# The local transformer of a twelve-layer kernel, with its instruction order given as cyclic lists per engine

## The chip, the core and the metric

The kernel runs on one core of a Trainium2 chip. TensorE (PE) multiplies matrices and writes to PSUM, whose eight banks hold 128 x 512 float32 each; VectorE (DVE), ScalarE (ACT) and GpSimd (POOL) work element by element; SyncE (SP) issues the DMAs. Each engine works through its own instructions in order and waits on semaphores for the others. The metric is the time of one execution in microseconds on the device, as a median of several runs.

## The reference

Everything is float32; activations are (8, 256, 128). Twelve layers of four families follow each other, each added to its input: mixture of experts, attention, mixture of experts; two-branch feed-forward, RWKV-6, two-branch feed-forward; **local transformer**, attention, **local transformer**; mixture of experts, attention, mixture of experts. The change touches only the two local transformers. Each runs six layers (`DEPTH = 6`) of this, with 16 heads of 64 and windows of 32:

```python
def attn_layer(x, Wqkv, qs, ksc, Wo):
    q, k, v = split(x @ Wqkv)                     # 128 -> 3 x 1024
    q = l2norm(q) * qs
    k = l2norm(k) * ksc
    q = q * cos * scale + rotate_half(q) * sin * scale
    k = k * cos * inv + rotate_half(k) * sin * inv
    # each window of 32 queries looks at its own and the previous 32 keys
    sim = einsum('bhwie,bhwje->bhwij', q, k2) * 8 ; mask ; softmax
    return einsum('bhwij,bhwje->bhwie', attn, v2) @ Wo

def ffn_layer(x, g, bln, W1, b1, W2, b2):
    xn = (x - mu) / jnp.sqrt(var + 1e-05) * g + bln
    a, gate = split(xn @ W1 + b1)                 # 128 -> 2 x 341
    return a * gelu(gate) @ W2 + b2

for i in range(DEPTH):
    x = attn_layer(shift_tokens(x), ...) + x      # shift: half the channels move one token
    x = ffn_layer(shift_tokens(x), ...) + x
```

## The kernel before

Channels lie on partitions, tokens along the row. The eight sequences form four groups of two (`NG = 4`), so a tile of activations is 128 x 512. The layers are stages 0 to 11; the local transformers are stages 6 and 8, written by `ffn2`.

In a local stage the work is cut into **quads**: one layer, one group, four of the sixteen heads. Four quads and the output projection and feed-forward behind them are a **unit**; a stage has 6 x 4 = 24 units, 96 quads. A quad is this chain: projection of k and of q (`pp`, `quad_project`), squares on ACT, cosine product and partner shuffle on DVE, sine product and sum on POOL; sums of squares per head on PE (`bank`, `quad_norms`), their inverse roots on ACT (`quad_roots`, an Ln and an Exp), four small DMAs that bring the roots into `l_rt`, shuffles on DVE that spread them (`quad_pick`), scaling of k and q on POOL (`quad_keys`); value projection `vp`, copied on ACT into `l_v` and by two DMAs, moved by one window, into `l_w` (`quad_values`); scores `sc`, maximum and difference on DVE (`quad_scores`); exp on ACT (`quad_exp`); transposes `et`, copied on ACT into `l_at` (`quad_turn`); weighted values `cx` in two halves, each divided on DVE (`quad_weigh`); transposes back `ct`, copied on ACT into `l_ct` (`quad_back`, `quad_done`). Behind the fourth quad of a unit comes `local_rest`: the output projection `wo_acc` in three parts, the residual `x1`, the shift, the normalization (`mean`, `ln_c`, `ln_sq`, `var`, `lv`, `ln_r`, `t` and its affine), the three chunks of W1 with gelu (`ge`, `l_gl`, `l_ag`), W2 (`w_acc`) and the residual `x2`.

The order of the work is the order in which the program is written. `_Ordered` ties each instruction of PE, DVE, ACT and POOL to the one before it on that engine, so no scheduler moves it; the DMAs on SP are not tied. `ffn2` (line 1630) is a loop that takes one new quad per step and writes, in a fixed sequence of whole functions, a part of each of the last four quads: `q0` projections, norms, roots and values; `q1` picking, scaling and scores; `q2` exp, transposes and weighted values; `q3` transposes back. The rest of a unit is a generator whose pieces are written at four places of each step (`piece`), over four steps from the one in which its last quad is transposed back. Two of these places call `pump` where no piece is due or the piece leaves room, which writes the next bit of work of a neighbouring stage (the end of the one before, the normalization at the entrance of the one behind). `entered` calls `pump` until a group's input is there.

In PSUM a local stage has three tiles of two banks (`two`, shared by `pp`, `vp`, `sc`, `et`, `cx`, `ct`, `ge`), one bank for the norms and the pumped work, and one bank for `wo_acc`, `mean`, `var` and `w_acc`.

Because all instructions of a local stage go through `_Ordered`, they carry its line, L285, in the profile; the tile names tell them apart.

Of the kernel before, what the change touches and what calls it, by code (L numbers as in the profile page):

```python
# [28 lines left out]
P = 128  # L29
B, S, D = 8, 256, 128  # L30
NB = 2
# [262 lines left out]
class _Net:  # L294
# [952 lines left out]
    def local_rows(self):  # L1247

        gp = self.nc.gpsimd
        one = lambda n, i, shape: self.work(f"{n}{i}", shape, bufs=1)  # L1250

        self.xs = [one("l_xs", i, (P, T)) for i in range(4)]
        for t in self.xs:
            gp.memset(t[64:, 0::S], 0.0)
        self.n_pad = 0

        self.rt = one("l_rt", 0, (P, T))
        gp.memset(self.rt, 0.0)
        self.low_masks(("lrow", "lmask"))
# [37 lines left out]
    def quad_project(self, q, n):  # L1297

        nc = self.nc
        four = lambda a: a.rearrange("p j (b s) -> p (j b) s", b=NB)  # L1300
        o = S if n == "k" else 0
        pp = self.two("pp")
        for j in range(2):
            self.mm(pp[:, j, :], q.w[:, o + P * j : o + P * (j + 1)], q.xs)
        sq = self.work("l_sq", (P, 2, T), bufs=4)
        nc.scalar.activation(sq, pp, AF.Square)
        y = self.work("l_y" + n, (P, 2, T), bufs=2)
        nc.vector.tensor_tensor(four(y), four(pp), q.tab[n + "cos"], ALU.mult)
        yr = self.work("l_yr", (P, 2, T), bufs=2)
        nc.vector.stream_shuffle(yr, pp, [i ^ 1 for i in range(32)])  # L1310
        nc.gpsimd.tensor_tensor(four(yr), four(yr), q.tab[n + "sin"], ALU.mult)
        nc.gpsimd.tensor_tensor(y, y, yr, ALU.add)
        q.y[n], q.sq[n] = y, sq

    def quad_values(self, q):
        nc = self.nc
        vp = self.two("vp").rearrange("p a b -> p (a b)")
        for m in range(4):
            self.mm(vp[:, S * m : S * (m + 1)], q.xs[:, P * m : P * (m + 1)], q.w[:, 2 * S :])
        v, w = self.vs[q.n % 2]  # L1320
        nc.scalar.copy(v.rearrange("p m h d -> p (m h) d")[:, :, :64],
                       vp.rearrange("p (n d) -> p n d", d=64))
        nc.sync.dma_start(w[32:], v[:96])
        nc.sync.dma_start(w[:32, 1::2], v[96:, 0::2])
        q.v = (w, v)

    def quad_norms(self, q):  # L1330
        sp = self.ps()
        for s, (n, j) in enumerate((("k", 0), ("q", 0), ("k", 1), ("q", 1))):
            self.mm(sp[32 * s : 32 * s + 32, :], self.get("hsum"), q.sq[n][:, j, :])
        q.sums = self.work("l_rn", bufs=1)
        self.nc.vector.tensor_scalar(q.sums, sp, 1e-24, None, ALU.max)

    def quad_roots(self, q):
        nc = self.nc
        rn = q.sums
        self.act(rn, rn, AF.Ln, scale=2.0**SH)  # L1340
        self.act(rn, rn, AF.Exp, bias=self.get("eps", 3, 1), scale=-0.5)
        for s in range(4):
            nc.sync.dma_start(self.rt[s::32], rn[32 * s : 32 * s + 32 : 8, :])

    def quad_pick(self, q):
        nc = self.nc
        q.r = {}
        for n, o in (("k", 0), ("q", 1)):
            r = q.r[n] = self.work("l_sq", (P, 2, T), bufs=4)
            for j in range(2):  # L1350
                nc.vector.stream_shuffle(r[:, j, :], self.rt, [2 * j + o] * 32)

    def quad_keys(self, q):

        nc = self.nc
        q.kp = self.kp[q.n % len(self.kp)]
        seq = lambda a: a.rearrange("p j (b s) -> p (j b) s", b=NB)
        nc.gpsimd.tensor_tensor(q.kp[:, :, WIN:], seq(q.r["k"]), seq(q.y["k"]), ALU.mult)
        nc.gpsimd.tensor_tensor(q.y["q"], q.y["q"], q.r["q"], ALU.mult)

    def quad_scores(self, q):

        nc = self.nc
        sc = self.two("sc")
# [19 lines left out]
        sl = lambda a: a.rearrange("p (n k) -> p n k", k=64)  # L1384
        bc = lambda a: a.unsqueeze(2).to_broadcast([P, 16, 64])
        sv = sl(sc.rearrange("p h n -> p (h n)"))
        mx = self.work("l_mx", (P, 16), bufs=2)
        nc.vector.tensor_reduce(mx, sv, AX.X, ALU.max)
        e = self.work("l_e", (P, 2 * T), bufs=2)
        nc.vector.tensor_tensor(sl(e), sv, bc(mx), ALU.subtract)  # L1390
        q.e = e

    def quad_exp(self, q):
        self.act(q.e, q.e, AF.Exp)

    def quad_turn(self, q):

        nc = self.nc
        tp = self.two("et").rearrange("p a b -> p (a b)")
        for n in range(8):  # L1400
            nc.tensor.transpose(tp[:, P * n : P * (n + 1)], q.e[:, P * n : P * (n + 1)],
                                self.get("ident"))
        q.at = self.work("l_at", (P, 2 * T), bufs=1)
        nc.scalar.copy(q.at, tp)

    def quad_weigh(self, q):

        nc = self.nc
        q.cx = []
        for j in range(2):  # L1410
            cp = self.two("cx")[:, :, : 4 * 65].rearrange("p x (n d) -> p x n d", d=65)
            for b in range(NB):
                for h in range(2):
                    for jj in range(4):
                        for x in range(2):
                            ks = slice(64 * x, 64 * x + 64)
                            o = P * (4 * h + 2 * j + b) + 32 * jj
                            self.mm(cp[32 * jj : 32 * jj + 32, x, 2 * b + h, :],
                                    q.at[ks, o : o + 32],
                                    q.v[jj % 2][ks, 2 * b + jj // 2, 2 * j + h, :])  # L1420
            rc = self.work("l_rc", (P, 2, 4), bufs=2)
            nc.vector.reciprocal(rc, cp[:, :, :, 64])
            cx = self.work("l_cx", (P, 2, 4, 64), bufs=4)
            nc.vector.tensor_tensor(cx, cp[:, :, :, :64],
                                    rc.unsqueeze(3).to_broadcast([P, 2, 4, 64]), ALU.mult)
            q.cx.append(cx)

    def quad_back(self, q):

        nc = self.nc  # L1430
        tp = q.tp = self.two("ct")
        for j in range(2):
            to = tp[:, j, :].rearrange("p (b c x i) -> p b x c i", b=NB, c=2, x=2)
            for b in range(NB):
                for x in range(2):
                    nc.tensor.transpose(
                        to[:, b, x], q.cx[j][:, x, 2 * b : 2 * b + 2].rearrange("p h d -> p (h d)"),
                        self.get("ident"))

    def quad_done(self, q):  # L1440
        ct = self.work("l_ct", (P, 2, T), bufs=5)
        self.nc.scalar.copy(ct, q.tp)
        q.unit.ct.append(ct)

    def local_rest(self, u):


        nc, i = self.nc, u.i
        acc = self.bank1("wo_acc")

        def project(cs):
            for c in cs:
                self.mm(acc, u.w["wo"][:, c, :], u.ct[c // 2][:, c % 2, :], start=c == 0, stop=c == 7)

        project(range(3))
        yield False
        project(range(3, 6))
        yield False
        yield False
        project(range(6, 8))  # L1460
        u.x1 = self.new_x()
        nc.vector.tensor_tensor(u.x1, acc, self.ys[u.g], ALU.add)
        if i == DEPTH - 1 and u.g == NG - 1:
            self.rest = u
            return
        xs = self.shifted(u.x1)
        yield False

        yield False
        self.settle()  # L1470
        xc, r = self.scratch("ln_c"), self.scratch("ln_r")
        m = self.bank1("mean")
        self.mm(m, self.get("mean"), xs)
        nc.vector.tensor_tensor(xc, xs, m, ALU.subtract)
        sq = self.scratch("ln_sq")
        nc.scalar.activation(sq, xc, AF.Square)
        yield True
        yield True
        v = self.bank1("var")
        self.mm(v, self.get("mean"), sq)  # L1480
        self.rsqrt(r, v, 0)

        hn = self.scratch("t", bufs=2)
        u.early = [
            lambda: nc.vector.tensor_tensor(hn, xc, r, ALU.mult),
            lambda: nc.scalar.activation(hn, hn, AF.Identity, bias=self.get(f"F{i}_ln_b"),
                                         scale=self.get(f"F{i}_ln_g")),
        ]
        yield True
        for f in u.early:  # L1490
            f()
        u.early = []
        yield False
        yield True
        o = self.bank1("w2_acc")
        ags = []

        def second(m):
            f = GE_CHUNKS[m][1]
            self.mm(o, u.w["w2"][:f, m, :], ags[m][:f, :], start=m == 0, stop=m == 2)  # L1500

        def first(m):
            f, w = GE_CHUNKS[m]
# [318 lines left out]
```

## Time and profile before

| | |
|---|---|
| median of 3 runs | 5218.47 us (5218.33 to 5227.95) |
| span of the profiled execution, first to last instruction | 5219.8 us |
| stage 6 (local), first to last quad and its rest | about 955 to 2660 us |
| stage 8 (local) | about 2905 to 4600 us |
| PE busy in stage 6, stage 8 | 1609 of 1705 us, 1596 of 1695 us |
| DVE, ACT, POOL busy in stage 6 | 1332, 903, 1397 us |
| granted clock of PE, mean | 0.973 of full speed |

The two local stages are some 3400 of 5220 us. How to read what follows: a row of a timeline gives the start, the duration, the engine, the line and the operation, output tile before input tiles, the shape, and how many instructions were merged; in square brackets stands how long the engine had been idle before it and what ended the wait. A row of busy time by stretch gives for PE, weight loads, DVE, ACT and POOL the busy microseconds and the count of instructions, then the granted clock of PE, the share of the DMA engines and GB/s. A row of a group gives the total busy time, the mean of one in ns, and the idle time in front. A float32 matmul stands as two instructions in the profile.

### The profile page before, as it was taken

The page shows a single profiled execution, that of the slowest core. Times are in us where ns is not written, and L with a number is a line of the kernel's source. Part 1 is how long each engine was busy: PE and PEld are TensorE (multiplying, and loading weights), DVE is VectorE, ACT ScalarE, POOL GpSimd, SP SyncE. Part 2 cuts the span into 40 slices and gives each one's busy share as a digit, 9 for nine tenths or more (in the row PEclk, how much of TensorE's full clock was granted, in tenths as well). Part 3 has the DMA queues.
Part 4 walks back from the last instruction along what each step waited for, and adds up shares of the span by engine and source line. Part 5 has one row for each costly group of instructions (what it writes and reads, how often), then busy time and mean ns, then how long its engine had stood idle before and what let it go on. Part 6 is the DMA issues. An engine that isn't in the chain of part 4 may idle for free.

```text
span 5219.8 us, 156276 instructions
## 1 busy us (share of the span) xinstructions
PE 4887.5 (94%) x70032; PEld 2895.3 (55%) x70032; DVE 3599.4 (69%) x6390; ACT 2483.9 (48%) x3011; POOL 3033.2 (58%) x1543
## 2 busy tenths in 40 slices
PE   9999998899999999999988899999999999989889
PEld 6755764455555555555544455555555555555456
DVE  4445446777777877787745777877787778755655
ACT  2233225555555555555544455555555555543652
POOL 0011003688888887888720588888888888701520
PEclk9999998999999999999989999999999999999999
DMA  2000000111111111111000011111111111100000
GB/s 75 1 1 1 1 1 1 40 29 49 34 49 35 43 38 45 38 42 41 26 28 5 21 36 42 37 46 37 42 41 42 41 39 41 29 36 1 1 1 9
DMA packets 61390, 151.76 MB, mean 29 GB/s; under 512 B 11185, under 2 KB 25394, under 8 KB 60466
## 3 DMA queue, kind: packets, MB, share of 16 engines
q1 hardware_dynamic: 60722, 141.77, 8.9%
q8 instruction: 551, 9.03, 0.7%
q14 instruction: 117, 0.96, 0.1%
HBM read 44.93 MB, written 1.05 MB: 9 GB/s over the span
## 4 chain that ended last, share of the span: by engine, by line
PE 71%; DVE 14%; ACT 8%; issue 2%; POOL 1%; DMA 1%; SPq 1%; DVEq 0%; ACTq 0%; POOLq 0%
PE mm L340 11%; PE pp L285 8%; PE e_o L340 7%; PE wo_acc L285 7%; PE bank L285 6%; PE sc L285 5%; PE vp L285 5%; PE ge L285 5%; PE cx L285 3%; PE ct L285 3%; DVE l_sq L285 3%; PE w_acc L285 2%; DVE l_yr L285 2%; PE ms L285 2%; ACT l_ct L285 2%
## 5 line engine op out<-in xcount | busy, mean ns | idle before, releaser
L285 PE MATMUL pp<-l_xs,wqkv 128*128 128x512 f32 x1536 | 693.4, 594 | 5.5 <-DMA wqkv<-in_f_wqkv 3.8
L285 POOL TENSOR_TENSOR l_kp<-l_sq,l_yk 128x1024 f32<-128x1024 f32 x192 | 456.6, 2378 | 357.4 <-DVE l_sq L285 354.2
L285 ACT COPY l_v<-vp 128x1024 f32<-128x1024 f32 x192 | 194.6, 1014 | 693.5 <-PE vp L285 693.5
L285 DVE STREAM_SHUFFLE l_sq<-l_rt 128x512 f32<-128x512 f32 x768 | 515.7, 747 | 0.1
L285 DVE STREAM_SHUFFLE l_yr<-pp 128x1024 f32<-128x1024 f32 x384 | 510.2, 1329 | 0.0
L285 PEld LDWEIGHTS pp<-l_xs,wqkv 128*128 128x128 f32 x1536 | 292.6, 191 | 356.6 <-issue 327.2
L340 PE MATMUL mm<-x,m 128*128 128x512 f32 x1024 | 479.4, 608 | 0.0
L285 POOL TENSOR_TENSOR l_yq<-l_yq,l_sq 128x1024 f32<-128x1024 f32 x192 | 476.1, 2479 | 0.1
L285 POOL TENSOR_TENSOR l_yr<-l_yr,l_ksin 128x1024 f32<-128x1024 f32 x192 | 456.5, 2378 | 24.9 <-DVE l_yr L285 24.9
L285 POOL TENSOR_TENSOR l_yq<-l_yq,l_yr 128x1024 f32<-128x1024 f32 x192 | 455.0, 2370 | 15.1
L285 POOL TENSOR_TENSOR l_yk<-l_yk,l_yr 128x1024 f32<-128x1024 f32 x192 | 454.2, 2366 | 15.0
L285 POOL TENSOR_TENSOR l_yr<-l_yr,l_qsin 128x1024 f32<-128x1024 f32 x192 | 455.0, 2370 | 0.0
L285 DVE TENSOR_REDUCE l_mx<-sc 128x16 f32<-128x1024 f32 x192 | 235.1, 1225 | 277.1 <-PE sc L285 277.1
L285 ACT ACTIVATE l_sq<-pp 128x1024 f32<-128x1024 f32 x384 | 384.1, 1013 | 54.5 <-PE pp L285 54.2
L340 PEld LDWEIGHTS e_o<-m,e_h 128*128 128x128 f32 x3072 | 363.1, 192 | 60.8 <-issue 60.3
L285 PE MATMUL vp<-wqkv,l_xs 128*128 128x256 f32 x1536 | 388.4, 396 | 2.6 <-issue 1.6
L285 PE MATMUL bank<-l_sq,sb_cs 128*32 128x512 f32 x1536 | 305.0, 617 | 67.0 <-ACT l_sq L285 66.5
L340 PE MATMUL e_o<-m,e_h 128*128 128x128 f32 x3072 | 363.6, 275 | 0.0
L285 PE MATMUL wo_acc<-l_ct,wo 128*128 128x512 f32 x768 | 360.9, 603 | 2.3 <-issue 2.3
L285 PE MATMUL cx<-l_w,l_at 64*32 64x65 f32 x12288 | 312.2, 226 | 51.0 <-ACT l_ct L285 41.1
L285 PE MATMUL sc<-l_kp,l_yq 64*32 64x64 f32 x24576 | 312.2, 228 | 22.6 <-issue 14.3
L285 PE MATMUL cx<-l_v,l_at 64*32 64x65 f32 x12288 | 318.8, 227 | 3.1 <-issue 3.1
(316 smaller groups left out, 9566.9 us busy)
## 6 DMA issues: line engine op xcount, KB each, us to landing
l_w<-l_v SPq DMA_DIRECT2D x192, 390.0 KB
wqkv<-in_f_wqkv SPq DMA_DIRECT2D x48, 384.0 KB
l_w<-l_v SPq DMA_DIRECT2D x192, 65.0 KB
l_rt<-l_rn SPq DMA_DIRECT2D x768, 8.0 KB
wo<-in_f_wo SPq DMA_DIRECT2D x12, 512.0 KB
m<-in_m_w SPq DMA_DIRECT2D x16, 256.0 KB
w<-in_f_w SPq DMA_DIRECT2D x12, 341.0 KB
w<-in_f_w SPq DMA_DIRECT2D x12, 192.0 KB
```

What stands on the lines that cost most here:

```text
L285: r = f(*args, **kw)
L340: self.nc.tensor.matmul(out, lhsT=lhsT, rhs=rhs, start=start, stop=stop)
```

## The change

The work is the same, operation by operation; what is rewritten is the order. Each function of a quad and of a unit's rest is cut into single operations (`op_ppk`, `op_sqk`, `op_cosk` and so on; 36 for a quad, 30 for a unit). `ORDER` gives each engine a cyclic list. `ppk.1` means: in step t this engine does `ppk` of quad t - 1. Operations of a unit exist only for its last quad. `AFTER` says what must have been written before an operation can be written (an operation and how many quads back), `HELD` which operations free the PSUM place that one takes. `ffn2` fills one queue per engine and step and writes from the head of each queue whatever is ready, until nothing moves; then it calls `pump` once. So the program order on each engine is its list, repeated.

```diff
+    ORDER = {
+        "PE": (
+            "ppk.1 mean.6 ppq.1 w20.7 wo1.5 ge2.7 ctp.5 wo0.4 var.6 norms.1 vp.3 cx1.4 "
+            "cx0.4 sc.2 ge1.6 ge0.6 wo2.5 w21.7 et.3"
+        ),
+        "ACT": (
+            "tab1.7 gl1.7 gl0.7 at.4 sqk.1 lsq.6 sqq.1 gl2.7 tab2.7 lln.6 ct.5 lex.6 "
+            "exp.3 v.3 aff.6 rln.1 rex.1 inA.0 xsA.5"
+        ),
+        "DVE": (
+            "x2.8 x1.6 qshuf.2 ag0.7 kshuf.2 xc.6 cosk.1 shufk.1 cosq.1 shufq.1 ag2.7 "
+            "hn.6 nmax.1 d1.4 d0.4 max.2 sub.2 ag1.6"
+        ),
+        "POOL": (
+            "xsP.6 kadd.2 kscale.2 qscale.2 inP.1 ksin.1 qsin.1 qadd.1"
+        ),
+        "DMA": (
+            "vs.4 rt.1"
+        ),
+    }
+    AFTER = {
+        "ppk": "inA.1 inP.1",
...
+        "norms": "sqk.0 sqq.0",
...
+        "at": "et.0 cx0.1 cx1.1",
...
+        "rt": "rex.0 kshuf.1 qshuf.1",
+    }
+    HELD = {
+        "ppk": ("psp2", "sqk cosk shufk"),
...
+        "sc": ("psp2", "sub"),
+        "norms": ("bank", "nmax"),
+        "wo0": ("acc", "x1"),
...
+    }
+    PLACES = {"psp2": 3, "bank": 1, "acc": 1}
...
     def ffn2(self):
...
-        while True:
-            q0 = next(gen, None)
...
-            if q1:
-                self.quad_pick(q1)
-            if q1:
-                self.quad_keys(q1)
...
-            self.piece(pieces, True)
-            q1, q2, q3 = q0, q1, q2
+        t, last = 0, max(k for l in order.values() for _, k in l)
+        while t < total + last or any(queues.values()):
+            for e, l in order.items():
+                queues[e].extend((o, t - k) for o, k in l if exists(o, t - k))
+            moved = True
+            while moved:
+                moved = False
+                for e in order:
+                    while queues[e] and ready(*queues[e][0]):
+                        emit(*queues[e].popleft())
+                        moved = True
+            if self.set == LN_EXP:
+                self.pump()
+            t += 1
```

What the short names mean: `sqk`, `sqq` squares; `cos`, `shuf` cosine product and partner shuffle from PSUM; `ksin`, `kadd` sine product and sum on POOL; `nmax` the floor under the norms on DVE, `rln`, `rex` the roots on ACT, `rt` their four DMAs, `kshuf`, `qshuf` the shuffles that spread them, `kscale`, `qscale` the scaling; `vp`, `v`, `vs` values, copy and its DMAs; `max`, `sub`, `exp` softmax; `et`, `at` transposes and copy; `cx0`, `cx1`, `d0`, `d1` weighted values and division; `ctp`, `ct` transposes back and copy. Of a unit: `wo0` to `wo2`, `x1`; `xsA`, `xsP` the shift for the feed-forward on ACT and POOL, `inA`, `inP` that for the next unit's input; `mean`, `xc`, `lsq`, `var`, `lln`, `lex`, `hn`, `aff` the normalization; `ge0` to `ge2`, `gl`, `ag`, `w20`, `w21`, `x2`; `tab1`, `tab2` the loads of the activation tables.

Buffers change in part with it: three tiles instead of four for the shifted inputs; one tile each for the squares of k and q and for the spread roots of k and q, in place of four shared ones; one partner tile for k and one for q, in place of two shared ones; own tiles for the feed-forward's normalization (`l_lc`, `l_lr`, `l_hn`) in place of shared scratch tiles (`ln_c`, `ln_sq`, `lv`, `ln_r`, `t`), in which `lsq`, `lln` and `lex` work in place; `ag` is written over `gl`.

The weights of the next layer are loaded when the last unit of a layer has used them for the last time (`next_weight`, and `quad_weights` in `op_vp`); before, three of the four were loaded in the first units of the layer that needs them. Those of the first layer are loaded at the start of the stage.

## The prediction

> **What bounds the kernel now.** The page first: busy time by engine.
>
> ```profile
> PE 4887.5 (94%) x70032; PEld 2895.3 (55%) x70032; DVE 3599.4 (69%) x6390; ACT 2483.9 (48%) x3011; POOL 3033.2 (58%) x1543
> ```
>
> TensorE leads by far. The change touches only the two local stages (about 955 to 2660 and 2905 to 4600 us), so I then took busy time by stretch in the middle of the second one, where neither fill nor drain is inside, and the groups of instructions of the same stretch.
>
> ```profile
> 3100.00:4300.00 1200.00, 1145.26 (x21341) 664.81 (x21340) 954.90 (x1596) 641.72 (x746) 1004.20 (x451) 0.99 0.14 41
> ```
>
> ```profile
> L285 PE MATMUL pp<-l_xs,wqkv 128*128 128x512 f32 x552 | 248.1, 592 | 0.0
> ...
> L285 DVE TENSOR_TENSOR t<-ln_c,ln_r 128x512 f32<-128x512 f32 x18 | 36.9, 2052 | 0.0
> ...
> L285 DVE TENSOR_TENSOR ln_c<-l_xs,mean 128x512 f32<-128x512 f32 x18 | 12.2, 678 | 0.0
> ```
>
> A quad issues 8 of the pp matmuls, so 552 are 69 quads in 1200 us: 17.39 us a quad, 69.6 us a unit of four quads with its feed-forward. Per unit (1200/69.6 = 17.25 units) PE is busy 66.4 us, POOL 58.2, DVE 55.4, ACT 37.2. PE idles 3.2 us a unit, but its 66.4 is not all work. The timeline of PE gives what its work takes when nothing holds it; I read start to start, since a matmul's end overlaps the next.
>
> ```profile
> 3423.55 2.74 PE L285 MATMUL wo_acc<-l_ct,wo 128*128 128x512 f32 x6
> 3426.12 1.04 PE L285 MATMUL et<-sb_c,l_e 128*128 128x128 f32 x8
> 3427.09 1.06 PE L285 MATMUL bank<-l_sq,sb_cs 128*32 128x512 f32 x8
> 3428.09 1.09 PE L285 MATMUL ct<-sb_c,l_cx 128*128 128x128 f32 x8
> ...
> 3430.53 2.84 PE L285 MATMUL wo_acc<-l_ct,wo 128*128 128x512 f32 x6
> 3433.30 0.39 PE L285 MATMUL sc<-low_lmask,low_lrow 64*128 64x512 bf16 x2
> 3433.62 1.49 PE L285 MATMUL sc<-l_kp,l_yq 64*32 64x64 f32 x128
> 3435.04 1.99 PE L285 MATMUL vp<-wqkv,l_xs 128*128 128x256 f32 x8
> 3436.87 1.88 PE L285 MATMUL wo_acc<-l_ct,wo 128*128 128x512 f32 x4
> 3438.59 3.60 PE L285 MATMUL pp<-l_xs,wqkv 128*128 128x512 f32 x8
> 3442.02 1.04 PE L285 MATMUL et<-sb_c,l_e 128*128 128x128 f32 x8
> ```
>
> Per quad: pp 3.43, et 0.97, norms (bank) 1.00, ct 1.02, both cx 1.42, sc 1.74, vp 1.83: 11.41 us. Per unit besides: wo 2.57 + 2.77 + 1.72, mean 1.06, var 0.86, ge 3.64 + 1.72, w2 0.86 + 1.92 (from the same timeline): 17.12. A unit is 4 x 11.41 + 17.12 = **62.8 us** of PE, 6.8 under the 69.6 it takes. The largest single piece of the 6.8 comes once a unit:
>
> ```profile
> 3457.98 1.04 PE L285 MATMUL bank<-l_sq,sb_cs 128*32 128x512 f32 x2
> 3462.27 1.58 PE L285 MATMUL bank<-l_sq,sb_cs 128*32 128x512 f32 x6 [3.25 <-ACT l_sq L285]
> 3463.78 1.97 PE L285 MATMUL ct<-sb_c,l_cx 128*128 128x128 f32 x8
> ```
>
> ```profile
> 3458.00:3462.00 4.00, 1.02 (x3) 0.11 (x2) 4.00 (x6) 1.51 (x2) 4.00 (x2) 1.00 0.00 0
> ...
> 3464.00:3466.00 2.00, 2.00 (x32) 1.67 (x39) 1.75 (x2) 0.21 (x1) 1.92 (x2) 0.50 0.00 0
> ```
>
> The norm matmuls wait 3.25 us for the square on ACT, which stands behind the feed-forward's affine, which waits for DVE's t (2.05 us), behind the shuffles, behind the DMA of the roots. Afterwards the granted clock is 0.50 and ct takes 1.97 instead of 1.09. So the old order pays twice: a wait, and slow matmuls after it. The rest are shorter waits in most quads: the second half of cx for the copy of ct, whose PSUM slot it takes (0.31, in 52 of the 69 quads), and norms for the second square.
>
> **The change, part by part.** No instruction is added or removed; each engine gets a cyclic list, and parts of a quad are spread over five steps instead of four, the feed-forward over steps 4 to 8 after its quad. In the steady state PE runs four kinds of step, by the unit work in them: a (wo0) 13.98 us, b (wo1, wo2) 15.90, c (mean, var, ge1, ge0) 16.97, d (w20, ge2, w21) 15.91: 62.8. The question is who makes PE wait in the new order. I set the engines' lists against each other from the start of a at 0 (b 13.98, c 29.88, d 46.85), with durations from the trace.
>
> *Removed waits.* Norms now follow ctp and the unit work, 1 us or more after the second pp; the square (0.95 us after ppq) is ready. Between ctp and cx stand norms and vp, 2.8 us, so the copy of ct (1.0) is hidden. The affine stands behind v on ACT, after both squares. That takes away 3.25 and the clock loss, and the 0.3s.
>
> *The roots' trip* (ACT roots, DMA, DVE shuffles) must now fit beside one step. Its price today:
>
> ```profile
> 3381.68 0.54 SPq L1343
> 3382.33 0.54 SPq L1343
> ...
> 3383.45 1.64 DMA l_rt<-l_rn
> ```
>
> Roots end at 3381.66, data at 3385.09, shuffles start at 3385.38: 3.7 us. In step a vp ends at 9.85, v on ACT at 11.0, both roots at 12.4, data at 16.1. DVE then shuffles (2.58) and does cosine and partner shuffle of k and q (4.72): 23.4, and cx0 of step b, which takes the PSUM slot that the last of them frees, has its turn at 24.7. Margin 1.3. In d vp takes that slot: 54.9 against 55.3, margin 0.4; c and a have more.
>
> *POOL* is in order: after qshuf and kshuf at 18.7, kscale, qscale, inP, ksin, qsin, qadd (five of 2.33 to 2.44 and 0.6) end at 31.2 and the shift for the feed-forward (xsP, 0.6) at 31.8. mean's turn on PE is 31.6: a **new wait of 0.25**. Behind mean stand ppq and the whole step. POOL's total of 58.2 stays under 62.8.
>
> *Feed-forward in c:* xc 33.1 to 33.75 (kshuf ends 33.1), var on PE ends 36.5, ln, ct and exp on ACT to 38.9, hn 39.0 to 41.0, affine 41.85; ge1's turn is 42.5, margin 0.65. Behind hn on DVE stand nmax, both divisions, max, sub: sub ends 45.9, et's slot is wanted at 46.1, margin 0.25. *In d* ppq takes ge0's slot, freed by ag0 behind qshuf: 48.9 against 48.8, a **new wait of 0.15**.
>
> *Edits at nothing:* single tiles for squares, partners and spread roots (the previous use is over: kadd frees the partner tile at 34.3, shufk wants it at 34.9; without that margin shufk waits, and vp behind it). v's second copy goes behind the four root DMAs on SP's queue; it is wanted 6 us later. Layer weights are fetched when the last unit frees them, on SP behind that step's roots and ahead of the next v; each is wanted four steps later. Table loads stay two a unit.
>
> *Sum.* 62.8 + 0.4 new waits + 0.5 (the idle put down to "issue" in front of sc, cx and wo, 8.1 us in the 1200, or 0.47 a unit, which no order removes) + 0.5 for margins of 0.25 that I do not trust = 64.2 us. That is 5.4 less a unit. First and last unit of each stage are fill and drain, with the same chains in both orders: 44 of 48 units count, 44 x 5.4 = 238. The queue of the neighbouring stages' work is served once a step, not up to twice; forced norms at the three later groups' entries may show; bounds 0 to 40 (six entries of one norm chain of about 6.5 us), I take 4. 5219.8 - 238 + 4 = 4986, say **4985 us**. The span of the profiled execution is 1.3 us above the median of the three runs, so no correction.
>
> [...]
>
> **Rivals.** *The roots' trip gets longer (slower).* The 390 KB copy of v is issued right when the roots start, about 1.4 us ahead of the first root DMA; before, it went 10 us or more ahead (3421.36 and 3431.54 in one quad). If the small DMAs queue behind it, DVE, then POOL and PSUM slots are late. For x us more, mean waits x more (through POOL), c x - 1.3, d x, a x - 2. The gain of 5.4 is gone at x = 2.2, a trip of 5.9 us; at 2.5 the waits are 2.5 + 1.2 + 2.5 + 0.5 = 6.7, the unit 70.9, 44 x 1.3 + 4 = 61 us more: **5281**. Against it: one v copy with a 384 KB load beside it kept the DMA engines busy for only some 3.6 us (DMA share by half microsecond), and the last root DMA is issued 2.2 us after the first.
>
> *The feed-forward's chain in c is late (small gain).* xc, square, var, ln, exp, hn cross three engines within one step. If hn ends 3 us later (a full POOL instruction and a late lex), PE waits 2.75, and 1.3 more go to the clock as today: 68.2, 1.4 x 44 = 62: **5162**. For it: margins of 0.25 and 0.65. Against: nothing in the trace makes these operations longer than I took.
>
> *It does not do what it says:* lists fix the order in the program, not when buffers come free; the lost waits return elsewhere in equal size: **5219**.
>
> **Numbers.** Forecast 0.68, own range 4900 to 5080: the floor itself, 62.8 on 46 units, is 5219.8 - 46 x 6.8 = 4907; the top is 1 us more trip (about 2 us a unit). Small gain 0.15, slower 0.11, nothing 0.06. Range 4900 to 5180: it leaves out the slow rival and tails. 0.2% is 10 us, about what a measurement of this kernel can tell from no change: faster 0.68 + 0.14 + 0.02 = 0.84, same 0.01 + 0.03 = 0.04, slower 0.11 + 0.01 = 0.12.
>
> **What would show it.** After: about 16.0 us a quad in mid-stage; PE's wait on l_sq in front of bank gone and its clock at 1.00 all through; PE busy up to about 98% there; ct at 1.09 everywhere. If mean waits for l_xs, POOL is late; if cx or ppq wait for DVE, the trip is longer than 3.7; if ge or et wait, it is the feed-forward. I am wrong if quads still take over 17 us, or if the first 100 us of the stages lose what the middle wins.

## The result and the profile after

The changed kernel takes **5393.33 us** (median of 4 runs, 5362.31 to 5399.04) against 5220.93 us before (4 runs, 5218.33 to 5227.95): ratio 1.0316, interval 1.0287 to 1.0345. It is 172 us slower; forecast was 235 us faster. The profiled execution has a span of 5397.1 us.

First the waits of PE over the whole execution: what it waited for, us in total, how often, the longest. Before:

```profile
PE bank L285 <- ACT l_sq L285: 66.5, 44, 3.8
PE cx L285 <- ACT l_ct L285: 41.1, 134, 0.3
...
PE sc L285 <- issue: 14.3, 27, 1.6
```

After:

```profile
PE sc L285 <- issue: 271.4, 169, 2.9
PE et L285 <- DVE l_rc L285: 36.3, 11, 5.6
```

The two waits that the change was forecast to remove are gone: no wait of the norms (bank) for the squares or of cx for ct is left in the list. In their place stands one that was in the profile of before with 14 us and is now 271 us: PE idle in front of sc, with nothing in the trace that it waited for.

The middle of the second local stage, PE, weight loads, DVE, ACT, POOL, then the granted clock, and groups of PE from the same stretch (the last figures are the idle time ahead):

```profile
3200.00:4400.00 1200.00, 1085.37 (x20539) 639.00 (x20538) 953.18 (x1541) 625.21 (x722) 964.54 (x436) 0.97 0.13 39
```

```profile
L285 PE MATMUL pp<-l_xs,wqkv 128*128 128x512 f32 x536 | 250.0, 604 | 0.8 <-issue 0.8
...
L285 PE MATMUL sc<-l_kp,l_yq 64*32 64x64 f32 x8521 | 118.2, 228 | 93.8 <-issue 93.5
...
L285 PE MATMUL w_acc<-l_gl,w 128*128 128x512 f32 (+1 forms) x98 | 56.7, 690 | 1.3 <-issue 1.3
```

The last of these groups in the kernel before:

```profile
L285 PE MATMUL w_acc<-l_ag,w 128*128 128x512 f32 (+1 forms) x108 | 54.1, 610 | 0.0
```

536 pp matmuls are 67 quads: 17.91 us a quad and 71.6 a unit, against 17.39 and 69.6 before and 64.2 forecast. The 93.5 us are 5.6 us a unit (16.75 units). The clock fell from 0.99 to 0.97, and the large matmuls are slower in the mean: pp 604 ns for 592 before, w_acc 690 for 610. With ge (631 for 601) and wo (612 for 599) that is 24 us of the stretch, 1.4 us a unit. One stall in the timeline of PE:

```profile
3413.04 0.39 PE L285 MATMUL sc<-low_lmask,low_lrow 64*128 64x512 bf16 x2
3413.36 1.21 PE L285 MATMUL sc<-l_kp,l_yq 64*32 64x64 f32 x100
3415.90 0.45 PE L285 MATMUL sc<-l_kp,l_yq 64*32 64x64 f32 x28 [1.33 <-issue]
```

sc is cut in two: its matmuls run, PE stops 1.33 us, and the rest follows. Its operands were there, since its first part ran. So no buffer and no semaphore explains it. In the new order cx1, cx0 and sc follow each other directly; each small float32 matmul shows as two matmuls and two weight loads, 256 instructions in cx and 260 in sc. Before, a piece of unit work stood between cx and sc in 175 of the 192 quads; now sc follows cx directly in 187.

**Theory A:** PE's instructions arrive at a limited rate, and this run of short ones outpaces it. **Theory B:** the fetches of instructions are held up by the 390 KB copy of v, which SP issues 1.0 to 2.1 us ahead of the five stalls between 3390 and 3470 us. **The rival:** the loss comes from the other new waits and the lower clock, and the stalls are only a symptom.

### The profile page after: what moved, and what is told of

The parts are those of the page before. It is cut to its first block, busy times and chain, and to the rows that moved or that the text cites. A ratio compares the mean times of both kernels' runs of the same rounds, so it can differ in the third digit from the quotient of the medians.

```text
span 5397.1 us, 156167 instructions
## 1 busy us (share of the span) xinstructions
PE 4860.2 (90%) x70032; PEld 2900.0 (54%) x70032; DVE 3681.7 (68%) x6390; ACT 2488.0 (46%) x3011; POOL 3018.4 (56%) x1541
## 5 line engine op out<-in xcount | busy, mean ns | idle before, releaser
L285 POOL TENSOR_TENSOR l_kp<-l_nk,l_yk 128x1024 f32<-128x1024 f32 x192 | 455.2, 2371 | 575.5 <-DVE l_nk L285 564.1
L285 PE MATMUL sc<-l_kp,l_yq 64*32 64x64 f32 x24576 | 340.5, 230 | 282.2 <-issue 271.4
L285 POOL TENSOR_TENSOR l_rq<-l_rq,l_qsin 128x1024 f32<-128x1024 f32 x192 | 474.5, 2471 | 0.0
L285 PEld LDWEIGHTS sc<-l_kp,l_yq 64*32 64x32 f32 x24576 | 279.0, 107 | 354.9 <-issue 335.0
L285 POOL TENSOR_TENSOR l_rk<-l_rk,l_ksin 128x1024 f32<-128x1024 f32 x192 | 456.0, 2375 | 10.1 <-DVE l_rk L285 10.1
L285 POOL TENSOR_TENSOR l_yq<-l_yq,l_rq 128x1024 f32<-128x1024 f32 x192 | 451.1, 2349 | 15.1
L285 POOL TENSOR_TENSOR l_yq<-l_yq,l_nq 128x1024 f32<-128x1024 f32 x192 | 456.7, 2378 | 0.0
L285 POOL TENSOR_TENSOR l_yk<-l_yk,l_rk 128x1024 f32<-128x1024 f32 x192 | 454.5, 2367 | 0.0
L285 ACT COPY l_at<-et 128x1024 f32<-128x1024 f32 x192 | 194.4, 1013 | 452.5 <-PE et L285 451.4
L285 PEld LDWEIGHTS vp<-wqkv,l_xs 128*128 128x128 f32 x1536 | 277.0, 190 | 190.3 <-issue 156.2
L340 PEld LDWEIGHTS mm<-x,m 128*128 128x128 f32 x1024 | 190.8, 195 | 201.3 <-issue 174.8
```

The lines of the kernel that those rows point to most:

```text
L285: r = f(*args, **kw)
L340: self.nc.tensor.matmul(out, lhsT=lhsT, rhs=rhs, start=start, stop=stop)
```

## The experiments

Times of `before` beside these runs were 5218.76 to 5221.48 us. Stalls always means the idle time of PE in front of sc that is put down to issue, in the whole execution.

**1. vp between cx and sc.**

```diff
-norms.1 vp.3 cx1.4 cx0.4 sc.2
+norms.1 cx1.4 cx0.4 vp.3 sc.2
```

> The changed kernel with the value projection (vp, 8 large matmuls, 1.99 us) moved in PE's list from ahead of cx to between cx and sc; nothing is left out. Theory A (PE's instructions do not arrive fast enough where cx, 256 instructions, and sc, 260, follow each other within 3.2 us): the idle time of PE in front of sc put down to issue falls from 271 us to under 60, and the time from 5393 to between 5090 and 5190. Theory B (the fetches of instructions are held up by v's 390 KB copy, issued about 1.3 us ahead of each stall): the copy moves along with vp, so this run does not decide on B. Rival (the loss comes from other waits: DVE's division ahead of et, xs ahead of mean, the late feed-forward, and the slower clock that follows): 5340 or more.

5295.28 us, ratio 1.0144 (1.0129 to 1.0159). The stalls are gone, 7.7 us, but two waits of PE take over:

```profile
PE sc L285 <- DVE l_cx L285: 156.2, 53, 8.4
PE vp L285 <- DVE l_rq L285: 56.3, 74, 1.5
```

sc now takes the PSUM slot of cx1 and waits for DVE's division; vp takes the slot of the second pp and waits for its shuffle. So the size was missed by 100 us, for a reason that is no theory's: moving an operation moves the slots too.

**2. Without v's copies.** `op_vs` returns for all but the first two quads of a stage.

> The changed kernel, which leaves out the two copies of v by DMA from the third quad of a stage on (the moved half of the values then stays that of the first quads); order unchanged. Theory A: the stalls in front of sc stay, over 200 us of them, and the time between 5340 and 5400. Theory B: the stalls fall under 60 us and the time to between 5090 and 5190. Rival (other waits): 5370 to 5400.

5323.48 us, ratio 1.0198 (1.0180 to 1.0216).

```profile
PE sc L285 <- issue: 251.4, 166, 3.0
```

The list of PE's waits has 251 of the 271 us of stalls left without the copies: theory B falls as the cause. The time, 17 us under theory A's range, is still 70 us lower, 20 of them stalls. The mean granted clock is 0.963 against 0.955, which is in the direction of the other 50; why it is higher was not followed further.

**3. Unit work between cx and sc in each step.**

```diff
-ctp.5 wo0.4 var.6 norms.1 vp.3 cx1.4 cx0.4 sc.2 ge1.6 ge0.6 wo2.5 w21.7 et.3
+ctp.5 var.6 norms.1 vp.3 cx1.4 cx0.4 wo0.4 ge1.6 ge0.6 wo2.5 w21.7 sc.2 et.3
```

> The changed kernel with the large matmuls of the unit (wo0, or ge1 and ge0, or wo2, or w21: one of them in each step) between cx and sc, and sc behind them just ahead of et; vp stays ahead of cx. Nothing is left out. Theory A: the idle time put down to issue in front of sc falls from 271 to under 60 us, the time to between 5080 and 5200. Theory B: v's copy is issued as before, but sc comes 1.7 to 3.7 us later and mostly meets the end of it: a smaller gain, 5150 to 5300. Rival (other waits): 5340 or more.

5496.51 us, ratio 1.0526 (1.0509 to 1.0544): the slowest, although the stalls fall to 21.9 us. What PE waits for instead:

```profile
PE et L285 <- DVE l_e L285: 119.6, 46, 2.7
PE ge L285 <- ACT l_hn L285: 80.3, 46, 1.9
PE mean L285 <- POOL l_xs L285: 60.6, 46, 4.1
```

The step with mean and var has no room: ge1 comes before its input is normalized, sc comes 3.7 us later, and et waits for DVE behind it. The expected time was missed by 300 us; only the prediction on the stalls held.

**4. The kernel before, with cx and sc side by side.**

```diff
             if q2:
                 self.quad_weigh(q2)
+            if q1:
+                self.quad_scores(q1)
             self.piece(pieces, True)
             self.piece(pieces)
-            if q1:
-                self.quad_scores(q1)
```

> The kernel before, with one edit: sc right behind cx, ahead of the two pieces of unit work that stood between them. vp, v and v's copy still come after. Theory A: stalls in front of sc put down to issue appear, from 14 us to between 100 and 280, and the time rises from 5219 to between 5270 and 5420. Theory B and the rival: v's copy is not nearer to sc than before, the idle time in front of sc stays under 40 us, and the time within 25 us of 5219.

5422.41 us, ratio 1.0391 (1.0373 to 1.0409).

```profile
PE sc L285 <- issue: 206.5, 176, 2.0
```

The same view of this kernel, against 14.3 us in the kernel before. It is the clearest run: nothing of the change is in it but the neighbourhood, and 14 us of stalls become 206, the time 202 us longer. v's copy comes after sc here. (The edit also brings var 48 us of waiting for its square, and takes 56 us off the norms' wait.) The stalls here are 2.0 us at most, and the granted clock, 0.972, is as before (0.973).

**5. The changed kernel with half as many, twice as wide matmuls** (the core of the edit; sc likewise):

```diff
-                        self.mm(cp[32 * jj : 32 * jj + 32, x, 2 * b + h, :],
+                    self.mm(cp[32 * jj : 32 * jj + 32, x, 2 * b : 2 * b + 2, :],
```

> The changed kernel, all orders as they are, with half as many and twice as wide small matmuls in cx and sc: each matmul of cx takes the weights of its first head for both heads, each of sc the queries of the first window for both windows, so as many columns go through PE with 260 instead of 516 instructions; what the second head and window should have had is left out. Theory A (too many instructions in too little time): the idle time put down to issue in front of sc falls from 271 to under 30 us, PE's clock returns to 0.98 or more, and the time comes to between 5030 and 5150. Theory C (the order itself holds sc up, by a semaphore or a buffer that the trace calls issue): the stalls stay over 200 us and the time above 5340.

4970.84 us, ratio 0.9522 (0.9508 to 0.9536). No stall in front of sc is left among the waits, so theory C, which the expectation names, falls: the order is unchanged. The largest waits in the local stages are now:

```profile
PE et L285 <- DVE l_rc L285: 64.0, 11, 6.5
PE mean L285 <- POOL l_xs L285: 53.9, 36, 4.4
```

It is faster than expected, since the wide matmuls also cost less (cx some 0.3 us and sc as much a quad). What that is worth, the next run shows. The expected clock of 0.98 shows in the local stage only (0.98 from 3200 to 4400 us, 0.966 over the whole). Queue 8 of the DMA queues (packets, MB, share) carries instructions. After, and in this run:

```profile
q8 instruction: 551, 9.03, 0.7%
```

```profile
q8 instruction: 359, 5.88, 0.5%
```

192 packets fewer, and 192 quads of 256 instructions fewer: exactly 256 PE instructions a packet. The queue is PE's: 551 packets are 141 056 instructions, and the profile has 140 064 matmuls and weight loads.

The traces also hold the start and length of each packet, and these settle theory A. In the stall shown above PE stops at 3414.57 us, a packet that started at 3413.59 lands at 3414.54, and PE goes on at 3415.90. So it is with all 169 stalls of the changed kernel: each ends 1.1 to 1.7 us behind the landing of a packet, 1.4 in the median, though packets land only every 8 us in the median. In run 4 the 176 stalls end 1.2 to 1.7 us behind one. And in none of the 17 runs do two packets start less than 3.2 us apart (3.37 in the changed kernel): 256 instructions in 3.4 us is the fastest seen there, where cx and sc use up 256 in 1.6 us. Run 2 has the same spacing (3.21) without v's copies.

**6. The kernel before with the same matmuls.**

> The kernel before with the same half as many, twice as wide matmuls in cx and sc; the same is left out. Theory A: it had 14 us of such stalls in sc and 7 in cx and loses those at most: between 5190 and 5225. Then the difference to the changed kernel with the same matmuls is what the order alone is worth without the stalls, some 80 to 190 us by theory A. Theory C: both kernels keep their distance, this one some 170 us ahead.

5133.42 us, ratio 0.9829 (0.9813 to 0.9846). It gains 88 us, more than the 31 at most that were expected: the cheaper matmuls, which the expectation had left out. With equal matmuls the new order is **162.6 us ahead** (4970.84 against 5133.42); with the original ones it is 172.4 us behind. The swing of **335 us** is the price of the short matmuls side by side: 257 us are the stalls themselves (271 against 14), and slower matmuls at 1.4 us a unit would be, by estimate, some 65 more. It is not exact, because other waits grew in both kernels as the matmuls got shorter (here the norms' from 66.5 to 104.7 us and cx's from 41.1 to 60.4). With runs 4 to 6 the rival falls: the neighbourhood alone makes the stalls and the loss, and without the stalls the new order is ahead.

**7. A mix:** wo0, wo2 and w21 between cx and sc, ge1 and ge0 behind sc.

```diff
+norms.1 vp.3 cx1.4 cx0.4 wo0.4 wo2.5 w21.7 sc.2 ge1.6 ge0.6 et.3
```

> The changed kernel with wo0, wo2 and w21 moved in PE's list to stand between cx and sc; ge1 and ge0 stay behind sc, so three of the four steps have large matmuls in between and the one with mean and var has none. Nothing is left out. Theory A: stalls stay in one step of four: issue in front of sc between 80 and 130 us of the 271, the time between 5190 and 5270. Theory C: over 200 us and above 5340.

5286.04 us, ratio 1.0129 (1.0114 to 1.0144). Stalls of 81.1 us in 61 places, as expected; the time is above the range, because mean now waits 59.9 us (45 times) for POOL's shift and et 58.2 us (11 times, once a layer) for DVE. The latter is the four scale tables of the next layer, 2.16 to 2.50 us each on DVE, one behind the other ahead of d1.

**8. Fewer matmuls in cx alone.**

> The changed kernel with half as many, twice as wide matmuls in cx alone (the second head's weights are left out): 388 instructions in the 3.2 us of cx and sc. Theory A: at a rate of 256 instructions in some 2.35 us the third block comes about 0.4 us late or not late at all: issue in front of sc between 20 and 130 us, the time between 5090 and 5240. Theory C: over 200 us and above 5340.

5083.05 us, ratio 0.9735 (0.9721 to 0.9750), stalls 73.3 us in 64 places, as expected (the time is 7 us under its range): 388 instructions lie between 260 (none) and 516 (271 us).

**9. The mix with the tables spread and x1 early.** One table behind `nmax` of four earlier quads; `x1.5` ahead of `max` on DVE, `xsP.5` ahead of `qadd` on POOL.

> The kernel with wo0, wo2 and w21 between cx and sc (the mix), and two waits of it taken away: the four scale tables of the next layer are made one at a time behind the norms' maximum of four earlier quads, instead of all four (9.5 us of DVE) at once ahead of d1, and x1 with its shift on POOL goes ahead of the last sum of the step before. Nothing is left out. Theory A: et's 58 us behind l_rc and mean's 60 us behind l_xs mostly go, the 81 us of issue stalls in the step with mean and var stay: between 5150 and 5210, ahead of both kernels. If the waits only move to the next operation: 5260 or more.

5213.25 us, ratio 0.9987 (0.9978 to 0.9996). Both waits are gone, 73 us with them, and the time is 3 us above the range; stalls are 93.4 us and var now waits 49.1 us for its square.

**10. et ahead of sc as well** (at on ACT in the same step).

> The same, with et (8 transposes, 1.04 us) also ahead of sc, and at on ACT at the end of the same step: in the step with mean and var these 1.04 us then stand between cx and sc. Theory A: the issue stalls fall from 81 to between 20 and 60 us and the time is 15 to 50 us under the previous kernel's. Against it: sc now takes the PSUM slot of cx1 and may wait for DVE's division where hn is late, as it did where vp was moved; then it is 0 to 60 us slower than the previous kernel.

5237.58 us, ratio 1.0036 (1.0024 to 1.0048). Stalls 13.8 us, but sc waits 105.8 us for DVE's division in the slot of cx1: the objection held.

**11. Norms ahead of var** (from 9).

> The kernel with the spread tables and one more edit: the norm matmuls (1.06 us, no wait in this step) go ahead of var, which waits 1.1 us for the square on ACT in 46 units, 49 us in all. Nothing is left out. Expected: var's wait falls under 10 us, the issue stalls of 93 us stay, and the time falls by 30 to 50 us to between 5163 and 5185. If the wait only moves to ge, because var is no earlier: 5200 or more.

5233.83 us, ratio 1.0028 (1.0016 to 1.0041), a miss. var's wait falls to 8.8 us and the stalls to 54.2, but sc waits 41.3 us for ACT's copy of v and the norms 34.8 for the square. The waits add up to what they were; why it is 20 us slower stays open.

**12. Run 5 with the tables spread and x1 early** (`x1.5` here behind `sub`).

> The changed kernel with half as many, twice as wide matmuls in cx and sc (leaving out the second head's weights and the second window's queries) and with the spread tables and the early x1 besides; the rest of the order is the changed kernel's. If the tables (64 us in front of et, 12 in front of ge) and the late shift (54 us in front of mean) are what still kept it from the forecast, the time falls from 4971 by 90 to 130 us to between 4840 and 4880. If these waits only move on: above 4930.

4979.00 us, ratio 0.9536 (0.9517 to 0.9554): no gain over run 5. The waits moved on: et 37.9, ge 35.3, mean 34.1, var 21.8, vp 14.1 us. In mid-stage (3050 to 4050 us) PE is 95% busy and DVE and POOL 91% each: with PE fed, taking away one wait shows the next.

**13. As many matmuls, each twice as wide.**

```diff
-                        self.mm(cp[32 * jj : 32 * jj + 32, x, 2 * b + h, :],
+                        self.mm(cp[32 * jj : 32 * jj + 32, x, 2 * b : 2 * b + 2, :],
```

> The changed kernel with as many small matmuls in cx and sc as it has, each twice as wide (each writes both heads', or both windows', columns, the later over the earlier; the result is left out): 516 instructions as before, but cx and sc together about 2.1 us longer a quad by the rows of the kernels with wide matmuls. If instructions arrive at a limited rate, about 256 in 2.35 us: these use 516 in some 5.3 us, no faster than that, so the issue stalls in front of sc fall from 271 to under 60 us, and 192 quads of 2.1 us more, less some 330, make between 5390 and 5520. If it is the count, or the order, that stalls: the stalls stay over 200 us and the time is above 5700.

5443.66 us, ratio 1.0438 (1.0419 to 1.0456).

```profile
PE sc L285 <- issue: 170.9, 160, 2.6
```

The stalls lie between the two expectations, the time in the range of the first. From the start of cx to what follows sc the trace gives, for 516 instructions, 3.16 us at least and 4.98 in the median in the changed kernel, 4.26 and 5.53 here. So the work grew by 1.1 us, not 2.1, and half of that came out of the stalls. It is a rate more than a count. The expectation's 256 in 2.35 us, 109 a microsecond, was an estimate (516 in 3.16 us of work and a stall of 1.6 in the mean, 271.4 us in 169, give about as much) and too much: packets 3.4 us apart bring 76, and even at twice the width 256 are used up in 2.1 us. As 516 still pass in some 5 us, a part of them must, by these numbers, have landed before; how large a part is not shown.

**14. xc ahead of the k shuffles** (from 9).

```diff
-qshuf.2 ag0.7 kshuf.2 xc.6 cosk.1
+qshuf.2 ag0.7 xc.6 kshuf.2 cosk.1
```

> The kernel with the spread tables, and xc on DVE ahead of the shuffles of k instead of behind them (1.3 us earlier), so that the square for var is earlier; nothing is left out. var's wait for the square falls from 49 to under 15 us; if it does not only move on, the time falls by 25 to 50 us from 5213, to between 5163 and 5188; if it does, 5200 or more.

**5193.51 us**, ratio 0.9951 (0.9934 to 0.9967): ahead of both kernels, with nothing left out. var's wait is 6.3 us; vp's for a shuffle, 30.5 us, is new, and 87.2 us of stalls remain. The gain of 20 us is just short of the 25 expected.

**15. No step with cx and sc side by side** (from 10, with xc early, ge1 and ge0 ahead of sc and ag1 ahead of max).

> The kernel with et ahead of sc, with xc early as in the run before, and in the step with mean and var ge1 and ge0 ahead of sc too, with ag1 ahead of max on DVE; nothing is left out. No step then has cx and sc side by side: issue in front of sc stays under 15 us, sc's 106 us behind DVE's division shrink to under 50, and ge waits up to 1 us a unit for hn's affine. Between 5150 and 5215 from 5238; if pp then waits for DVE's ag1, above 5230.

5267.10 us, ratio 1.0093 (1.0075 to 1.0112). The stalls fall to 6.8 us and sc's wait for the division to 47.1, as expected, but the time is a miss: ct 37.4, vp 37.2 and pp 32.2 us now wait for DVE and ACT. Without the stalls an order is not yet a fast one.

## Why the prediction was wrong

**The step that failed** is the term "0.5 (the idle put down to "issue" in front of sc, cx and wo, 8.1 us in the 1200, or 0.47 a unit, which no order removes)". It took the idle time for a constant of the kernel. It depends on the order: the row of before was small because unit work stood between cx and sc. The new order puts 516 short instructions side by side in every quad, and the term became 5.6 us a unit in stalls and 1.4 in slower matmuls. Run 4 shows that the neighbourhood makes it, the packets show what PE waits for, and runs 5 and 6 price it: some 335 of the 408 us between forecast and result. Setting the engines' lists against each other could not show it, since that gave each matmul its duration and took its instruction as there.

**The rest, some 70 us,** is that the order alone is worth 163 us (runs 5 and 6) and not 235. From the starts of sc, a quad in mid-stage takes 15.84 us in run 5 and 16.85 in run 6: 4.0 us a unit for the 5.4 of the sum, some 60 us. In run 5 et waits 64, mean 54 and ge 12.5 us, 2.7 us a unit, where the sum had 0.9 (0.4 new waits, 0.5 margins). Et's is the four tables on DVE, which the prediction had not priced at all; mean's 54 us are 1.1 a unit for the 0.25 in the sum. But in run 12 the waits of et and mean fall to 37.9 and 34.1 us, others grow, and the time is no shorter, so what holds run 5 there is not shown.

**The stages' ends** were taken at 4 us. Of the 177 us between the spans of the two kernels, the steady pace (18.17 and 17.99 us a quad in stages 6 and 8, before 17.38 and 17.32) makes 140 on 192 quads; some 37 lie outside it. The first 16 quads of stage 6, from sc to sc, take 306.8 us, before 275.7. That points to the prediction's second sign of being wrong, the first 100 us of the stages; what is late there was not followed.

**Removed waits: right.** The norms' 66.5 us and cx's 41.1 us are gone. "Its clock at 1.00 all through" failed with the stalls.

**The roots' trip: right, and its rival falls.** DVE's wait for the spread roots, in the same 1200 us as above:

```profile
DVE l_nq L285 <- DMA l_rt<-l_rn: 0.8, 3, 0.3
```

0.8 us in 67 quads. v's copy in front of the root DMAs did no harm there, although the stalls also gave the trip time: in run 5, without them, DVE waits 20.4 us for the roots in 1000 us (41 times, 1.1 us at most).

**hn: the row was the wrong one.** The prediction gave hn the 2.05 us of its row of before (39.0 to 41.0 in c). hn in the whole execution, in the changed kernel and in run 14 (mean in ns after the bar):

```profile
L285 DVE TENSOR_TENSOR l_hn<-l_lc,l_lr 128x512 f32<-128x512 f32 x46 | 113.8, 2474 | 12.6 <-ACT l_lr L285 12.6
```

```profile
L285 DVE TENSOR_TENSOR l_hn<-l_lc,l_lr 128x512 f32<-128x512 f32 x46 | 40.5, 881 | 6.4 <-ACT l_lr L285 6.4
```

The same instruction, 2.47 us or 0.88. In the timeline of after one hn of 2.85 us starts 0.06 us behind a POOL instruction that lasts 2.37. Before, each of the 46 ends 0.54 to 0.55 us behind the end of the POOL instruction that ran when it started, with 1.3 us of that instruction left in the median. In the changed kernel 44 of the 46 end 0.55 to 0.66 us behind it, with 2.3 us left in the median, and the two that start while no POOL instruction runs last 0.69 us. In run 14 nearly all end behind it too, and in the median only 0.3 us are left. So in nearly all of these hn lasts as long as POOL's instruction still runs, and about 0.55 us more; why is not shown. It cost PE nothing (ge waits 0.6 us in the 1200, for the division), and not because of the stalls: in run 5, which has none, 11 of the 46 hn take over 2.3 us, and ge never waits for the affine behind them.

**The feed-forward's chain in c and "nothing changes"** did not decide: neither ge nor var is among the waits of after with more than 0.6 us in that stretch. The 172 us lost are not old waits come back in equal size, as the latter had it: the old ones are gone and a new one stands there.

## What to carry to other kernels

Idle time put down to issue was a property of the neighbourhood here (14 us in the kernel before, 206 in run 4), so before long runs of short matmuls are put side by side, count their instructions: here 516 took 5 us in the median, where PE could do them in 3.2, and 260 in 2.6 us made no stall. Put large matmuls between such runs, those that no chain waits for. And price an order by what each engine must be fed with too, not by durations and semaphores alone; where every engine is tight, each operation moved also moves the PSUM slots behind it.

## What the runs showed that was not expected

PE's instructions came in packets of 256 that started 3.37 us apart at the closest in the changed kernel, and its short matmuls used one up in some 1.6 us (516 in 3.16 us). What follows the longer stops was slower too: in the trace of after, 25 of the 30 stops of 2.0 us or more in front of sc are followed within 3.5 us by a stretch at half the clock, but only 22 of the 139 shorter ones, and w_acc, which stands behind sc, took 690 ns for 610. In run 4, with stops of 2.0 us at most, the clock was as before. Spread over a quad, the same instructions cost next to nothing (14 us of stalls in the kernel before), and a queue that took 0.7% of the DMA engines' time held the kernel up for 271 us.
